# A selective-scan stack: the norm's factor spread by two transfers and multiplied in by GpSimd, the ffn's inner values in their own buffer, z projected a piece ahead

## The chip, the cores and the metric

The kernel runs on one core of a Trainium2 chip. A core has a matrix engine (TensorE, PE in the profile; its weight loads are PEld), a vector engine (VectorE, DVE), an engine for activation functions (ScalarE, ACT), a general one (GpSimd, POOL), and a fifth that only issues transfers (SyncE, SP). Each has its own queue of instructions and works through it in order; semaphores hold an instruction until what it needs is there. Sixteen DMA engines move data between HBM (DRAM) and the core's memory (SBUF); PE writes its results into PSUM. The metric is device time in microseconds (us).

## The reference, cut to what matters

The input is x of shape (2, 128, 64, 64). Four stages follow one another: the layers (this document's subject), two attentions over the picture, and a fusion of four scales. The layers, cut:

```python
t = (embed_w @ x + embed_b)                   # per image: 4096 tokens of 128 channels
for i in range(2):                            # two layers
    r = t
    t2 = layernorm(t) * ln_g[i] + ln_b[i]
    u, z = split(t2 @ in_w[i].T)              # 256 channels each
    u = silu(causal_conv4(u))
    dt, B, C = split(u @ xproj_w[i].T)        # 8, 16, 16 values
    dt = softplus(dt @ dt_w[i].T + dt_b[i])
    h[t] = exp(dt * A) * h[t - 1] + dt * u * B    # 256 x 16 states, along the tokens
    y = (h * C).sum(states) + u * ssm_D
    t = (y * silu(z)) @ mout_w[i].T + r
    r = t
    t2 = layernorm(t) * ln_g[i] + ln_b[i]
    t = gelu(t2 @ ffn_w1[i].T + ffn_b1) @ ffn_w2[i].T + ffn_b2 + r
x = x + (outc_w @ t + outc_b)
```

The norm is over the 128 channels: (x - mean) / sqrt(var + eps).

## The kernel before

**Tiling.** Channels lie on the 128 partitions and tokens along the free dimension, in pieces of 512. An item is one piece of one layer of one image: 2 images x 2 layers x 8 pieces = 32 items. The 256 x 16 states of an item are handled as 8 groups (NST) of four scans each, 128 partitions x 512 tokens per scan, so an item has 32 slots (NSL), one scan each. All data are fp32, and each matrix product appears in the trace as two matmul records.

**Order.** The order of all instructions is written out by hand. `slot` (L565) issues, for slot t: at the first slot of a group the transfers `dtb` that spread dt (L401) for three groups later, the product `pdu` (L406) for the next group, and in every second group the sums `py` (L445) of an earlier pair of groups; then the scan on DVE (L430); then on ACT the decay `da` for the scan four slots later (L419; four PSUM buffers); at the last slot of a group, after the scan, POOL copies the carry (L432) and multiplies h by C (L433, "the h product"), and DVE makes the next group's h out of B and pdu (`times_b`, L412). After that come the slot's entries of a list that `background` (L512) fills by hand with `at(slot, function, ...)`. pdu has one PSUM buffer (pool `l0bc`), so the product for the next group waits for times_b to have read the last. Since every engine keeps this order, an entry that waits holds up all that its engine has behind it.

**The list.** While step i scans item i, the list does for item n = i + 1 the input product with the convolution folded in (`pu`, slots 0 to 5), silu (11), `xproj` (13), the transfers `dr`, `bb`, `cb` that spread B and C over the partitions (14 and 22), `dtproj`, softplus (17) and dtu on POOL (18); for item i the product `pz` (slots 1 and 5, copied by ACT in 3 and 6); for item p = i - 1 the output `y_out`, gate and mix (7 to 11); for item q = i - 2 gelu (3), the ffn's second product (6, 7) and its sum. The products of the list share two PSUM buffers (tag `mm`).

**The norm.** Two norms go together in each step: the second norm of item p (result x2, for the ffn) and the first of item r = i + 2 (result xn). PE centres (12, 14), ACT squares (13, 15), PE makes the variances of both in a 2-row product (17), ACT adds eps (18, `ln_eps`), takes ln, exp and a square (19, `ln_rs`); one Newton step follows, with POOL and ACT in turn (20, 21). Then PE spreads each factor over the 128 partitions (`ln_spread`, L306, slot 27), DVE multiplies it in together with ln_g (`ln_scale`, L310, slot 28), and ACT adds ln_b (`ln_shift`, L323, slot 29). The ffn's first product `ph` (L478) and its copies into hid by ACT (L479) are in slots 30 and 31.

**Buffers.** h has a ring of five buffers (tag "h"), and hid, the ffn's inner values, takes one of the same ring in each step; for the last item it takes one of the attention's (tag "sc"). `xr`, the input for the last sum, has its own buffer.

Of the kernel before, what the change touches and what calls it, by code (L numbers as in the profile page):

```python
# [6 lines left out]
F32 = mybir.dt.float32  # L7
AF = mybir.ActivationFunctionType
ALU = mybir.AluOpType
# [6 lines left out]
P = 128  # L16
CH = 512
# [50 lines left out]
def tile_conv_seq(ctx: ExitStack, tc, x, consts, vecs, wemb, wlay, wconv, wdt, wqkv, wsmall, wms, out):  # L68
    nc = tc.nc
# [13 lines left out]
    def rows(ap):  # L83
        return ap.rearrange("p (h w) -> p h w", w=W)
# [19 lines left out]
    def v1(name, i=0):  # L104
        return vec[:, VEC[name] + i : VEC[name] + i + 1]

    def pick(row, k, m=P):

        return ident[:k, row : row + 1].to_broadcast([k, m])
# [6 lines left out]
    with tc.manual_schedule(), ExitStack() as s:  # L116
        wp = layers.enter_context(tc.tile_pool(name="l0w", bufs=1))
        spl = layers.enter_context(tc.tile_pool(name="l0t", bufs=1))
        mm = layers.enter_context(tc.tile_pool(name="l0mm", bufs=2, space=PSUM))
        yp = layers.enter_context(tc.tile_pool(name="l0y", bufs=1, space=PSUM))  # L120
        sp = scans.enter_context(tc.tile_pool(name="l0s", bufs=1, side="right"))
        bc = scans.enter_context(tc.tile_pool(name="l0bc", bufs=1, space=PSUM, side="right"))
        dap = scans.enter_context(tc.tile_pool(name="l0da", bufs=4, space=PSUM, side="right"))
        dp = s.enter_context(tc.tile_pool(name="l0d", bufs=2, space=bass.MemoryType.DRAM))
# [111 lines left out]
        NI, NST, NSL = len(items), 8, 32  # L236
        st = [{} for _ in items]
# [3 lines left out]
        def has(i):  # L241
            return 0 <= i < NI

        def vl(name, i, k=0):
            return v1(f"{name}{items[i][1]}", k)

        def tv(i):
            b, _, c = items[i]
            return xv(b, c)

        def mmt(name, p=P):
            return mm.tile([p, CH], F32, name=name, tag="mm")
# [27 lines left out]
                at = K_VS + 8 - k  # L280
                nc.tensor.matmul(var[:n], lhsT=kc[:, at : at + n], rhs=w["sq"][:, k, :], start=(k == 0), stop=(k == n - 1))

        def ln_eps(w, n):
            w["ve"] = spl.tile([2, CH], F32, name="ve", tag="ve")
            nc.scalar.activation(w["ve"][:n], w.pop("var")[:n], AF.Identity, bias=eps[:n])

        def ln_rs(w, n):
            w["rs"] = spl.tile([2, CH], F32, name="rs", tag="rs")
            nc.scalar.activation(w["rs"][:n], w["ve"][:n], AF.Ln)
            nc.scalar.activation(w["rs"][:n], w["rs"][:n], AF.Exp, scale=-0.5)  # L290
            w["nt"] = spl.tile([2, CH], F32, name="nt", tag="nt")
            nc.scalar.activation(w["nt"][:n], w["rs"][:n], AF.Square)

        def ln_newton(w, n):

            nt = w["nt"][:n]
            nc.gpsimd.tensor_tensor(nt, nt, w["ve"][:n], ALU.mult)
            nc.scalar.activation(nt, nt, AF.Identity, bias=c15[:n], scale=-0.5)

        def ln_step(w, n):  # L300
            rs = w["rs"][:n]
            nc.gpsimd.tensor_tensor(rs, rs, w["nt"][:n], ALU.mult)

        def ln_spread(w, k, n):
            w["pr", k] = mmt("pr")
            nc.tensor.matmul(w["pr", k], lhsT=pick(k, n), rhs=w["rs"][:n], start=True, stop=True)  # L306

        def ln_scale(w, k, i):
            cen = w["cen"][:, k, :]
            nc.vector.scalar_tensor_tensor(cen, cen, vl("ln_g", i), w.pop(("pr", k)), ALU.mult, ALU.mult)  # L310

        def ln_shift(w, k, i, second):
            if second:
                dst = st[i]["x2"] = spl.tile([P, CH], F32, name="x2", tag="x2")
            else:
                xn = st[i]["xn"] = sp.tile([P, KC - 1 + CH], F32, name="xn", tag="xn", bufs=2)
                if items[i][2] == 0:
                    nc.gpsimd.memset(xn[:, : KC - 1], 0.0)
                else:
                    nc.gpsimd.tensor_copy(xn[:, : KC - 1], prev_xn[0][:, CH : CH + KC - 1])  # L320
                prev_xn[0] = xn
                dst = xn[:, KC - 1 :]
            nc.scalar.activation(dst, w["cen"][:, k, :], AF.Identity, bias=vl("ln_b", i))  # L323


        def pu_taps(i, j, ks):
# [142 lines left out]
        def ffn_up(i, f):  # L469
            w = st[i]  # L470
            if f == 0:
                if i == NI - 1:
                    w["hid"] = spa.tile([P, 4, CH], F32, name="hid", tag="sc", bufs=3)
                else:
                    w["hid"] = sp.tile([P, 4, CH], F32, name="hid", tag="h", bufs=5)
            ph = mmt("ph")
            at = WL_W1 + f * P
            nc.tensor.matmul(ph, lhsT=wl[items[i][1]][:, at : at + P], rhs=w["x2"], start=True, stop=True)  # L478
            nc.scalar.activation(w["hid"][:, f, :], ph, AF.Identity, bias=vl("ffn_b1", i, f))  # L479
# [14 lines left out]
        def ffn_add(i):  # L494
            b, l, c = items[i]
            if l == NL - 1:
                xr = st[i]["xr"] = spl.tile([P, CH], F32, name="xr", tag="xr")
                nc.sync.dma_start(xr, x[b, :, c * RPC : (c + 1) * RPC, :].rearrange("c h w -> c (h w)"))
            nc.scalar.activation(tv(i), rows(st[i].pop("pf")), AF.Identity, bias=vl("ffn_b2", i))

# [11 lines left out]
        def background(i):  # L512

            todo = [[] for _ in range(NSL)]

            def at(t, f, *a):
                todo[t].append((f, a))

            n, p, q, r = i + 1, i - 1, i - 2, i + 2
            if has(q):  # L520
                at(3, gelu, q)
                at(6, ffn_down, q, (0, 1)), at(7, ffn_down, q, (2, 3)), at(9, ffn_add, q)
                at(11, out_mm, q), at(12, out_add, q)
            if has(p):
                at(7, y_out, p, 1), at(7, gate, p)
                at(9, mix_out, p), at(11, mix_add, p)
            if has(n):
                at(0, pu_taps, n, 0, (0, 1)), at(1, pu_taps, n, 0, (2, 3)), at(2, pu_out, n, 0)
                at(3, pu_taps, n, 1, (0, 1)), at(4, pu_taps, n, 1, (2, 3)), at(5, pu_out, n, 1)
                at(13, xproj, n), at(14, xproj_out, n), at(14, spread_bc, n, 0), at(22, spread_bc, n, 1)  # L530
                at(15, dtproj, n, 0), at(16, dtproj, n, 1), at(17, soft_plus, n), at(18, dt_end, n)
            if has(i):
                at(1, pz_mm, i, 0), at(3, pz_out, i, 0)
                at(5, pz_mm, i, 1), at(6, pz_out, i, 1)
            if has(i) or has(n):
                at(11, silu, i, n)
            if i == -1:
                at(1, load_rest), at(7, prepare, 1), at(9, through_out)
                for k in range(3):
                    at(8 + k, fold, k), at(23, fold_out, k)  # L540
                at(19, spread_dtu, 0), at(26, times_b, 0)
            pair = [(k, second) for k, second in ((p, True), (r, False)) if has(k)]
            if has(r):
                at(10, embed, r), at(11, embed_out, r)
            w, m = {}, len(pair)
            for k, (it, second) in enumerate(pair):
                at(12 + 2 * k, ln_centre, w, k, it)
                at(13 + 2 * k, ln_square, w, k, it)
                at(27, ln_spread, w, k, m), at(28, ln_scale, w, k, it)
                at(29, ln_shift, w, k, it, second)  # L550
            if pair:
                at(17, ln_var, w, m), at(18, ln_eps, w, m), at(19, ln_rs, w, m), at(20, ln_newton, w, m), at(21, ln_step, w, m)
            if has(p):
                for f in range(4):
                    at(30 + f // 2, ffn_up, p, f)
            if has(i):
                at(24, y_out, i, 0)
            return todo

        eps = wp.tile([P, 1], F32, name="eps")  # L560
# [21 lines left out]
        for i in range(-2, NI):  # L582
            todo = background(i)
            for t_ in range(NSL):
                slot(i, todo, t_)
        todo = background(NI)
        for t_ in range(8):
            slot(NI, todo, t_)
# [15 lines left out]
        spa = s.enter_context(tc.tile_pool(name="ata", bufs=1, reuse_waits="tile", side="right"))  # L604
# [297 lines left out]
        for k in range(8, 2 * NSL):  # L902
            if k == NSL:
                todo = background(NI + 1)
            for _ in range(int(beside[k - 8]) if k - 8 < len(beside) else 0):
                next(steps, None)
            slot(NI + k // NSL, todo, k % NSL)
# [4 lines left out]
        sp = s.enter_context(tc.tile_pool(name="ats", bufs=1, reuse_waits="tile"))  # L912
        psa = s.enter_context(tc.tile_pool(name="atpa", bufs=2, reuse_waits="tile", space=PSUM))
        psm = s.enter_context(tc.tile_pool(name="atpm", bufs=1, reuse_waits="tile", space=PSUM))
        for now in range(NALL + LAG + 8):
            r, u = divmod(now, NU)
            w = now % 8
# [64 lines left out]
    with ExitStack() as s, tc.manual_schedule():  # L982
        sp = s.enter_context(tc.tile_pool(name="mss", bufs=1, reuse_waits="tile"))
# [11 lines left out]
        for ti in range(NS):  # L995
            src = spr[:, ti, :].unsqueeze(2).to_broadcast([P, NH, HD])
# [27 lines left out]
        eps = sp.tile([P, 1], F32, name="eps")  # L1024
# [9 lines left out]
        for si in (2, 3):  # L1034
            wgt[si] = sp.tile([P, SCALES[si]], F32, name=f"wgt{si}")
            for k in range(SCALES[si]):
                w = (k + 0.5) / SCALES[si] - 0.5
# [5 lines left out]
        NI = len(items)  # L1043
        st = [{} for _ in items]
# [433 lines left out]
```

## Time and profile before

| what | us |
|---|---|
| median of 3 runs | 4975.6 (4974.84 to 4981.31) |
| the profiled execution's own time | 4975.69 |
| its span, first to last instruction | 4973.9 |
| layers, first scan to last scan (66.7 to 2094) | 2027 |
| PE busy in it | 1818 |
| DVE busy in it | 1883 |
| ACT busy in it | 1467 |
| POOL busy in it | 1428 |
| mean granted TensorE clock | 0.949 |

The profile is one execution, told by several views. A line of the timeline has start, length, engine, source line, operation, output and inputs with their shapes and the count; in brackets is the idle time of the engine before it, and what ended it. The chain of waits is followed back from the last instruction, at each step to what released it. "issue" is time in which nothing was waited for that the profile shows. A window has, after its length, the busy times of PE, PEld, DVE, ACT and POOL, with counts, then the granted clock of PE as a share of full speed, the share of the DMA engines in use, and GB/s. Line numbers are those of the kernel before.

### The profile page before, as it was taken

The numbers are of one execution on the slowest core, as the hardware profiler recorded it, in microseconds if no ns is written. First come the engines' busy times: TensorE is split into PE (matmuls) and PEld (weight loads), VectorE is DVE, ScalarE is ACT, GpSimd is POOL, SyncE is SP. The second block draws the span as 40 slices with busy tenths as digits, with TensorE's granted clock in tenths as the row PEclk, the third lists the DMA queues.
The fourth block names the chain that finished last, engine by engine and source line by source line (L and its number), as shares of the span: only waits on it lengthen the run. The fifth ranks groups of instructions, "written<-read, shape, count | busy, mean of one in ns | idle before, by whom it ended". The sixth has DMA issues, their size and how long they took to land.

```text
span 4973.9 us, 48435 instructions
## 1 busy us (share of the span) xinstructions
PE 4643.1 (93%) x14634; PEld 2218.0 (45%) x14634; DVE 3975.5 (80%) x4155; ACT 2361.8 (47%) x3225; POOL 2331.1 (47%) x1974
## 2 busy tenths in 40 slices
PE   6899999999988899899999999999999999999997
PEld 2222222222222222266667766666666666333332
DVE  6999999999999999878886677767766775667775
ACT  4677777777777777632222232233333332323332
POOL 3777776676777777613332233333333332334231
PEclk8888898988999989899999999999999999999998
DMA  6333332223333333214444444444444443000000
GB/s 163 68 67 68 69 69 67 67 67 71 69 69 69 71 73 71 69 36 126 113 111 123 113 109 115 122 99 111 114 101 98 114 112 83 3 7 7 7 5 9
DMA packets 242485, 386.28 MB, mean 78 GB/s; under 512 B 88608, under 2 KB 89136, under 8 KB 233776
## 3 DMA queue, kind: packets, MB, share of 16 engines
q1 hardware_dynamic: 193072, 316.01, 26.1%
q10 hardware_dynamic: 49152, 67.17, 5.4%
q8 instruction: 117, 1.92, 0.2%
q14 instruction: 144, 1.18, 0.1%
HBM read 101.09 MB, written 13.37 MB: 23 GB/s over the span
## 4 chain that ended last, share of the span: by engine, by line
PE 46%; POOL 25%; issue 12%; DVE 8%; DMA 4%; SPq 3%; ACT 3%; ACTq 0%; POOLq 0%; DVEq 0%
POOL h L433 19%; PE pq L780 13%; PE po L830 13%; DVE tr L810 3%; SPq L821 3%; DMA pt<-tr 3%; PE pa L677 2%; PE pf L1135 2%; PE pqkv L1162 2%; PE pw L1221 1%; POOL dtu L393 1%; POOL z L456 1%; PE pb L677 1%; PE pfus L1286 1%; PE psc L1186 1%
## 5 line engine op out<-in xcount | busy, mean ns | idle before, releaser
L817 POOL COPY pt<-tr 32x512 f32<-32x512 f32 x1024 | 644.7, 630 | 1410.8 <-DVE tr L810 700.7
L430 DVE TENSOR_TENSOR_SCAN h<-da,carry,h 128x512 f32<-128x512 f32 x1024 | 1241.6, 1265 | 65.1 <-ACT da L419 36.2
L433 POOL TENSOR_TENSOR h<-h,cb 128x2048 f32<-128x2048 f32 x256 | 1160.9, 4535 | 20.8
L780 PE MATMUL pq<-k,q 128*128 128x512 f32 x2048 | 963.4, 593 | 12.5 <-DVE sc L785 12.5
L830 PE MATMUL po<-pt,vt 128*128 128x256 f32 x4096 | 965.6, 379 | 3.5 <-POOL pt L817 3.5
L795 ACT ACTIVATE sc<-sc,nm 128x2048 f32<-128x2048 f32 x256 | 510.5, 1995 | 886.8 <-DVE nm L791 656.4
L830 PEld LDWEIGHTS po<-pt,vt 128*128 128x128 f32 x4096 | 777.9, 190 | 309.5 <-issue 227.5
L785 DVE TENSOR_SCALAR_CACHE_REDUCE sc<-pq 128x1024 f32<-128x1024 f32 x512 | 624.8, 1222 | 333.8 <-PE pq L780 311.7
L419 ACT ACTIVATE da<-dtb,am 128x512 f32<-128x512 f32 x1024 | 681.4, 684 | 221.3 <-DVE h L430 205.6
L412 DVE TENSOR_TENSOR h<-bb,pdu 128x2048 f32<-128x2048 f32 x256 | 581.4, 2271 | 85.4 <-PE py L445 28.3
L810 DVE STREAM_TRANSPOSE tr<-sc 128x2048 f32<-128x2048 f32 x256 | 591.6, 2311 | 65.7 <-DMA pt<-tr 59.3
L445 PE MATMUL py<-h,sel 128*32 128x512 f32 x2048 | 513.6, 645 | 1.8 <-POOL h L433 1.8
L780 PEld LDWEIGHTS pq<-k,q 128*128 128x128 f32 x2048 | 382.2, 190 | 291.5 <-issue 247.4
L406 PE MATMUL pdu<-dtu,fsel 128*128 128x512 f32 x512 | 327.8, 727 | 99.5 <-DVE h L412 97.5
L445 PEld LDWEIGHTS py<-h,sel 128*32 128x32 f32 x2048 | 115.6, 118 | 418.7 <-issue 413.1
L333 PE MATMUL pu<-xn,wu 128*128 128x512 f32 x512 | 245.9, 614 | 10.0 <-ACT u L339 8.3
L406 PEld LDWEIGHTS pdu<-dtu,fsel 128*128 128x128 f32 x512 | 96.6, 215 | 307.4 <-DVE h L412 180.5
L432 POOL COPY carry<-h 128x4 f32<-128x4 f32 x256 | 47.8, 187 | 390.3 <-DVE h L430 386.2
L1228 DVE TENSOR_TENSOR ov<-v,pw 128x2048 f32<-128x2048 f32 x64 | 146.2, 2284 | 65.1 <-PE pw L1221 65.1
L1162 PE MATMUL pqkv<-f,ws 128*128 128x512 f32 x384 | 188.8, 617 | 3.0 <-DVE prod L1179 2.3
L1232 POOL TENSOR_TENSOR ov<-ov 128x2048 f32<-128x2048 f32 x16 | 72.6, 4536 | 237.0 <-DVE ov L1228 237.0
L393 POOL TENSOR_TENSOR dtu<-dt,u 128x1024 f32<-128x1024 f32 x32 | 75.1, 2348 | 199.1 <-ACT dt L387 199.1
(265 smaller groups left out, 5152.4 us busy)
## 6 DMA issues: line engine op xcount, KB each, us to landing
pt<-tr SPq DMA_DIRECT2D x2048, 64.0 KB, 2.0
dtb<-dt SPq DMA_DIRECT2D x1024, 64.0 KB, 2.0
pt<-tr ACTq DMA_DIRECT2D x1024, 64.0 KB, 2.1
bb<-dr SPq DMA_DIRECT2D x128, 256.0 KB, 4.5
cb<-dr SPq DMA_DIRECT2D x128, 256.0 KB, 4.6
uw<-ufold SPq DMA_DIRECT2D x12, 576.0 KB, 4.4
uw<-dkept SPq DMA_DIRECT2D x20, 288.0 KB, 3.1
xt<-in_x SPq DMA_DIRECT2D x16, 256.0 KB, 4.8
```

The costliest lines, as they stand in the source:

```text
L406: nc.tensor.matmul(pdu, lhsT=four(s_ % 4), rhs=st[i]["dtu"][:, s_ // 4, :], start=True, stop=True)
L412: nc.vector.tensor_tensor(h, st[i]["bc", 0], pdu.unsqueeze(1).to_broadcast([P, 4, CH]), ALU.mult)
L419: nc.scalar.activation(da, st[i]["dtb", s_], AF.Exp, scale=am[items[i][1]][:, j, gg, m : m + 1])
L430: nc.vector.tensor_tensor_scan(h[:, m, :], da, h[:, m, :], carries[b, l][:, j, gg, m : m + 1], ALU.mult, ALU.add)
L433: nc.gpsimd.tensor_tensor(h, h, st[i]["bc", 1], ALU.mult)
L445: nc.tensor.matmul(py[r : r + 32, :], lhsT=sel, rhs=st[i]["h", s_ + k][:, m, :], start=(m == 0), stop=(m == 3), tile_position=(0, r),)
L780: nc.tensor.matmul(pq[:, i, :], lhsT=sta["q", r, grp][:, it * P : (it + 1) * P], rhs=sta["k"][:, at : at + CH], start=True, stop=True)
L785: nc.vector.tensor_scalar(dst, pq, 1.0, None, ALU.mult, ALU.max, accum_out=sta["mx"][:, c2 : c2 + 1])
L795: nc.scalar.activation(sc, sc, AF.Exp, bias=nm, scale=scale, accum_out=sm[:, hh : hh + 1])
L810: nc.vector.transpose(tr, sta.pop(("sc", r, blk, hh)).rearrange("p (t r f) -> p r t f", r=NB, f=32))
L817: nc.gpsimd.tensor_copy(dst, src)
L830: nc.tensor.matmul(sta["po", r, grp], lhsT=sta["vt"][:, jt, :], rhs=rhs, start=(jt == 0), stop=(jt == N // P - 1))
```

## The change

- `ln_eps` goes into `ln_rs`: ACT's four operations are issued together in slot 18. ve and nt lie in sq, which is free by then. The whole Newton step is in slot 19.
- `ln_spread` on PE goes. `ln_out` (slot 21) writes the factors (2 x 512) to DRAM; `ln_in` (slot 23) reads them back, each repeated for 128 partitions, into sq. Both are issued by SP.
- `ln_scale` is a product on POOL, without ln_g, in slots 25 and 27. ln_g is applied by ACT as the scale of `ln_shift`, for both norms in slot 28.
- hid has a buffer of its own in the pool of the layers. xr shares the buffer of x2.
- pz is made one item ahead: for n = i + 1, in slots 24 and 26, with its copies in 25 and 27.

```diff
-        def ln_eps(w, n):
-            w["ve"] = spl.tile([2, CH], F32, name="ve", tag="ve")
-            nc.scalar.activation(w["ve"][:n], w.pop("var")[:n], AF.Identity, bias=eps[:n])
-
         def ln_rs(w, n):
-            w["rs"] = spl.tile([2, CH], F32, name="rs", tag="rs")
-            nc.scalar.activation(w["rs"][:n], w["ve"][:n], AF.Ln)
-            nc.scalar.activation(w["rs"][:n], w["rs"][:n], AF.Exp, scale=-0.5)
-            w["nt"] = spl.tile([2, CH], F32, name="nt", tag="nt")
-            nc.scalar.activation(w["nt"][:n], w["rs"][:n], AF.Square)
+            ve, nt = w["sq"][:n, 0, :], w["sq"][:n, 1, :]
+            rs = w["rs"] = spl.tile([2, CH], F32, name="rs", tag="rs")
+            nc.scalar.activation(ve, w.pop("var")[:n], AF.Identity, bias=eps[:n])
+            nc.scalar.activation(rs[:n], ve, AF.Ln)
+            nc.scalar.activation(rs[:n], rs[:n], AF.Exp, scale=-0.5)
+            nc.scalar.activation(nt, rs[:n], AF.Square)
 
         def ln_newton(w, n):
-            nt = w["nt"][:n]
-            nc.gpsimd.tensor_tensor(nt, nt, w["ve"][:n], ALU.mult)
+            ve, nt, rs = w["sq"][:n, 0, :], w["sq"][:n, 1, :], w["rs"][:n]
+            nc.gpsimd.tensor_tensor(nt, nt, ve, ALU.mult)
             nc.scalar.activation(nt, nt, AF.Identity, bias=c15[:n], scale=-0.5)
-
-        def ln_step(w, n):
-            rs = w["rs"][:n]
-            nc.gpsimd.tensor_tensor(rs, rs, w["nt"][:n], ALU.mult)
-
-        def ln_spread(w, k, n):
-            w["pr", k] = mmt("pr")
-            nc.tensor.matmul(w["pr", k], lhsT=pick(k, n), rhs=w["rs"][:n], start=True, stop=True)
-
-        def ln_scale(w, k, i):
+            nc.gpsimd.tensor_tensor(rs, rs, nt, ALU.mult)
+
+        def ln_out(w, n):
+            w["rd"] = dp.tile([2, CH], F32, name="rd", tag="rd")
+            nc.sync.dma_start(w["rd"][:n], w["rs"][:n])
+
+        def ln_in(w, n):
+            src = w["rd"][:n].rearrange("(o k) f -> o (k f)", o=1)
+            nc.sync.dma_start(w["sq"][:, :n, :].rearrange("p k f -> p (k f)"), src.to_broadcast([P, n * CH]))
+
+        def ln_scale(w, k):
             cen = w["cen"][:, k, :]
-            nc.vector.scalar_tensor_tensor(cen, cen, vl("ln_g", i), w.pop(("pr", k)), ALU.mult, ALU.mult)
+            nc.gpsimd.tensor_tensor(cen, cen, w["sq"][:, k, :], ALU.mult)
...
-            nc.scalar.activation(dst, w["cen"][:, k, :], AF.Identity, bias=vl("ln_b", i))
+            nc.scalar.activation(dst, w["cen"][:, k, :], AF.Identity, bias=vl("ln_b", i), scale=vl("ln_g", i))
...
-                if i == NI - 1:
-                    w["hid"] = spa.tile([P, 4, CH], F32, name="hid", tag="sc", bufs=3)
-                else:
-                    w["hid"] = sp.tile([P, 4, CH], F32, name="hid", tag="h", bufs=5)
+                w["hid"] = spl.tile([P, 4, CH], F32, name="hid", tag="hid")
...
-                xr = st[i]["xr"] = spl.tile([P, CH], F32, name="xr", tag="xr")
+                xr = st[i]["xr"] = spl.tile([P, CH], F32, name="xr", tag="x2")
...
-            if has(i):
-                at(1, pz_mm, i, 0), at(3, pz_out, i, 0)
-                at(5, pz_mm, i, 1), at(6, pz_out, i, 1)
+                at(24, pz_mm, n, 0), at(25, pz_out, n, 0)
+                at(26, pz_mm, n, 1), at(27, pz_out, n, 1)
...
-                at(27, ln_spread, w, k, m), at(28, ln_scale, w, k, it)
-                at(29, ln_shift, w, k, it, second)
+                at(25 + 2 * k, ln_scale, w, k)
+                at(28, ln_shift, w, k, it, second)
             if pair:
-                at(17, ln_var, w, m), at(18, ln_eps, w, m), at(19, ln_rs, w, m), at(20, ln_newton, w, m), at(21, ln_step, w, m)
+                at(17, ln_var, w, m), at(18, ln_rs, w, m), at(19, ln_newton, w, m)
+                at(21, ln_out, w, m), at(23, ln_in, w, m)
```

## The prediction

> **What bounds the kernel now.** I read the page first, for the shares, then the chain of waits, then one round of the layers in the timeline, then the clock in windows, then the DMA issues. I look at the layers alone (up to about 2094 us of the span); the change touches nothing after them. From the page, the engines and the chain:
>
> ```profile
> PE 4643.1 (93%) x14634; PEld 2218.0 (45%) x14634; DVE 3975.5 (80%) x4155; ACT 2361.8 (47%) x3225; POOL 2331.1 (47%) x1974
> ...
> PE 46%; POOL 25%; issue 12%; DVE 8%; DMA 4%; SPq 3%; ACT 3%; ACTq 0%; POOLq 0%; DVEq 0%
> ```
>
> POOL is idle half of the time and yet holds a quarter of the chain: a loop passes through it. The chain in order of time (start, length, what), in the round of item 15:
>
> ```profile
> 1059.28 2.35 POOL dtu L393
> ...
> 1061.84 4.55 POOL h L433
> 1066.39 1.24 POOL nt L297
> ...
> 1068.28 0.68 ACT da L419
> ...
> 1068.98 1.26 DVE h L430
> ...
> 1072.61 2.19 DVE h L412
> 1074.80 0.04 issue
> 1074.85 2.08 PE pdu L406 x2
> 1076.92 5.21 PE py L445 x16
> 1082.13 3.82 PE ph L478 x8
> 1085.95 0.86 PE pdu L406 x2
> 1086.81 3.43 PE pu L333 x8
> 1090.24 0.87 PE pz L346 x2
> ```
>
> This is one round of a loop. Call D the start of dtu. POOL does dtu, the h product and nt; ACT's nt lets the next decay go; three scans and times_b follow on DVE; and only then may PE start pdu, because pdu has one PSUM buffer. From there PE works without a gap through py, ph, pu, pz, ffn, mix, centre and xproj; in the timeline softplus then ends 6.0 to 6.6 us after xproj, and the next dtu starts. The dtu starts are 172.67 and 2009.27 us for items 1 and 30: 29 rounds of 63.3 us, 61.7 to 65.1 each. In every round times_b of group 7 ends 15.5 us after D (call that point B) and pdu starts 0.05 us after it; what varies is PE after B. DVE is busy some 60 us of a round; its stalls (about 4.5 us) follow the loop rather than make it.
>
> ACT in the same round, from its timeline:
>
> ```profile
> 1067.65 0.72 ACT L298 ACTIVATE nt<-nt,c 2x512 f32<-2x512 f32 x1 [2.68 <-POOL nt L297]
> 1079.94 0.71 ACT L323 ACTIVATE xn<-cen,vec 128x512 f32<-128x512 f32 x1
> 1083.23 0.69 ACT L479 ACTIVATE hid<-ph,vec 128x512 f32<-128x512 f32 x1 [2.00 <-PE ph L478]
> ```
>
> xn is ready 5.8 us after B, and hid waits for PE: the norm has about 2 us to spare. The windows show the clock (the column after POOL) and the DMA share after it:
>
> ```profile
> 1056.30:1059.80 3.50, 2.27 (x6) 0.55 (x6) 3.19 (x2) 3.45 (x5) 0.52 (x1) 0.99 1.01 227
> 1059.80:1063.20 3.40, 3.40 (x6) 0.54 (x6) 3.38 (x4) 3.30 (x6) 3.32 (x3) 0.51 0.99 209
> 1070.00:1080.20 10.20, 8.70 (x14) 1.98 (x15) 10.10 (x10) 4.97 (x9) 9.22 (x4) 0.50 0.23 53
> 1080.20:1124.60 44.40, 43.16 (x116) 14.39 (x113) 39.61 (x29) 34.83 (x49) 26.21 (x13) 1.00 0.17 42
> ```
>
> A window with 1.23 us of idle PE is followed by one at half clock, and full clock returns only after a stretch of unbroken work. The second thing to see: while bb, cb and dtb land, all DMA engines are taken (0.99), at 209 GB/s. The issues, with the median time to landing:
>
> ```profile
> bb<-dr SPq DMA_DIRECT2D x128, 256.0 KB, 4.5
> cb<-dr SPq DMA_DIRECT2D x128, 256.0 KB, 4.6
> uw<-ufold SPq DMA_DIRECT2D x12, 576.0 KB, 4.4
> ```
>
> **The change, part by part**, for one round.
>
> *Removed from DVE and PE.* Two scale instructions on DVE (0.73 each) and two spreading products on PE (3.59 us cold, at 1069.76, between the loop's own pieces). Both lie off the loop, or before B where PE waits anyway: 0.
>
> *hid in its own buffer, ve and nt in sq, xr in x2's buffer.* The h ring keeps five buffers. DVE's waits at slots 31 and 7 (1.21 and 1.01 us for py, at 1082.23 and its like at 1032.67) go. They are shadows of PE's chain: y_out behind them waits for the same py. 0 on the loop. xr's load now waits for x2's last reader, a third of a round earlier: 0.
>
> *z a piece ahead.* The two pz in the PE stretch cost 0.94 each there (1090.08 to the next product at 1091.02); they move to slots 24 and 26, where PE idles before B: -1.9. Their copies on ACT go to slots 25 and 27, where ACT waits 2.9 and 1.8 us for scans: 0.
>
> *ve, ln, exp, square together; the Newton step a slot earlier.* The decay for scan 23 now stands behind ln, exp and square: 1.9 us later. More weighs that ACT's nt, which waits for POOL until 1067.65, now stands before the decay of scan 24 and not of scan 25. POOL's dtu, h and nt are the same, so scan 24 starts where scan 25 did, D + 9.7. From there: scan and y_out 1.9, three scans 3.55, times_b 2.26, so B is at D + 17.4 instead of D + 15.5: +1.9. The late scan 23 is covered (its times_b ends at D + 9 to 10).
>
> *Two transfers.* rs is ready at D + 10.4 (POOL 1069.71). ln_out is queued on SP ahead of cb, so cb, which went out at D + 3.8, now waits for rs too. It is needed only by the next item's first h product: 0. ln_out's 4 KB is taken at the 1.6 us of dr<-dbl (64 KB), landing at D + 12.1; cb's four issues take 1.9, so ln_in goes out at D + 12.75. It writes 512 KB. Alone it takes the 4.4 of uw<-ufold (576 KB): D + 17.15. Behind cb's 1 MB on full DMA engines, 1.5 MB at 209 GB/s take 7.5 us from D + 11.8: D + 19.4. The latter is nearer, since cb goes out just before it on the same queue. Call the landing B + 2.0; ends B - 0.25 and B + 2.6. The next dtb sit behind it on SP, needed 8 us later than they land: 0.
>
> *POOL's scale.* POOL's 2x512 product takes 1.26, and 128x1024 and 128x2048 (2.35, 4.54) lie on a line that gives 1.26 for 128x512. POOL would be free at B - 2.2; it waits, then scale 1.26, carry and h product 4.81, scale 1.26: B + 9.3. ACT's slot 28 holds both shifts, and in order behind them stand two decays and the first hid: 0.7 + 1.3 + 0.7, so hid ends at B + 12.05. PE has done py at B + 7.0 (rounds: 6.1 to 7.8) and two ph at B + 8.9; the third needs the buffer that hid empties (two PSUM buffers): PE waits 3.2 us, at the low end of ln_in 0.9, at the high end 3.8. pu needs xn (B + 10) anyway.
>
> *Clock.* By the row of 1056.30, a wait of this kind drops PE to half clock. The next two windows of 3.4 us hold the rest of the wait and some 4 to 5 us of work that then run at half: +1.9, between 0 and 3.4.
>
> Sum for a round: -1.9 + 1.9 + 3.2 + 1.9 = +5.1; 30 rounds: +153. At the head, item 0's norm sits on the path (rs 21.29, pu 25.10): out 1.6, in 4.4 and POOL 1.26 beside 3.0 for product and scale, and loads before them on SP: +7 (between 4 and 15). Tail: the last pr (2131.91) waits 6 us behind other products, which covers the transfers. The profiled execution took 4975.69 us, 1.8 around its 4973.9 span; the median is 4975.6, so no correction. 4975.7 + 160 = 5136.
>
> **Two rules beside the rows.** The Trainium skill, "DMA: Bandwidth & Descriptors", section "Anatomy of one DMA", gives 2.0 us plus bytes over 436 GB/s for a transfer (fitted on the GpSimd path). As an estimate ln_in would take 3.2 us, land at B - 1.45, and PE would wait nothing: 4983 by this sum. The rows show 209 GB/s with the engines full, so I keep the rows. The skill's "TensorE: Matmul & The Clock Gate", "Why this matters for your kernels", asks for no idle gap over about 3 us. By it most waits of 3.2 us or less would leave the clock alone: 5136 - 57 = 5079. The row with 1.23 us idle and 0.51 after it speaks against that.
>
> **Rivals.** (1) Faster: DVE is the true bound. Then 1.4 of scales and the waits of 1.2 and 1.0 come off each round: -3.6 x 30 = -108, 4868. For it: DVE is busy 93% of the layers. Against it: pdu follows times_b by 0.05 us in every round while DVE waits for py and pdu. It decides if PE's gaps between pdu and xproj turn out to be cover. A smaller form, PE kept at full clock by pz, would give up to -2.4 a round (py at B + 4.6), 4904; PE is idle over 5 us before B, against it. (2) The transfer is hidden: ln_in lands by B - 1.2, so that hid ends by B + 8.9, with the second ph. The round is then -1.9 + 1.9 = 0, with the head 4983. Against it: cb on the same queue. (3) ln_in is not queued behind cb and the clock holds: +0.9 a round, 5003 to 5010; this is the low end of my forecast.
>
> **How the numbers follow.** Within 0.2% (10 us) this kernel can't be told from no change. Chances: forecast with its low end (rival 3 included) 0.80; rival 2 0.09; rival 1 with its smaller form 0.11. Rival 2 ends on both sides of +0.2%, mostly within. So faster 0.12, same 0.07, slower 0.81. Upper end: 3.8 + 3.4 = 7.2 a round and 13 at the head, 5205. Lower end: rival 3 and part of rival 2, 4990. Outside lie rival 1 and what is over 7.2 a round, together under 0.2.
>
> **What would show it.** POOL's scale waits about 4 us for the DMA sq<-rd in each round; ACT's xn ends 9 to 10 us after B; PE's ph has an idle time of about 3 us before the third product, put down to ACT hid or xn; B lies 17.4 after D; rounds of 68 us; half clock in more windows after B. The prediction is wrong if sq<-rd lands before POOL's h product of group 5 ends, or if rounds fall to 60 us with DVE without gaps.

## The result, and the profile after

The changed kernel takes 5106.4 us (median of 4 runs, 5100.46 to 5109.29), the kernel before 4977.3 beside it (4974.84 to 4981.31): a ratio of 1.0257, with a 95% interval of 1.0239 to 1.0275. That is 129 us slower, where 160 were forecast. The profiled execution has a span of 5098.6 us, 124.7 more than before. From its page, the engines and the chain's shares:

```profile
PE 4605.2 (90%) x14506; PEld 2223.2 (44%) x14506; DVE 3939.6 (77%) x4091; ACT 2368.8 (46%) x3225; POOL 2405.5 (47%) x2038
...
PE 46%; POOL 19%; issue 12%; DVE 8%; DMA 6%; ACT 4%; SPq 3%; ACTq 0%; DVEq 0%; POOLq 0%
POOL h L431 13%; PE pq L775 13%; PE po L825 13%; DMA sq<-rd 3%; DVE tr L805 3%; SPq L816 3%; DMA pt<-tr 2%; PE pa L672 2%; PE pf L1130 2%; PE pqkv L1157 2%; POOL cen L308 1%; PE pw L1216 1%; PE pb L672 1%; POOL dtu L391 1%; PE pfus L1281 1%
```

PE and DVE have less to do than before and the program is longer, so both wait more. A line that before didn't have stands in the chain, DMA sq<-rd: ln_in, the transfer that spreads the norm's factor. One round of it, from the chain in order of time (start, length, what); D is at 984.73:

```profile
984.73 2.34 POOL dtu L391
...
991.78 1.27 POOL sq L294
...
993.08 0.73 ACT sq L295
...
993.87 1.26 POOL rs L296
...
995.27 0.12 SPq L300
...
997.30 6.30 DMA sq<-rd
...
1003.67 1.26 POOL cen L308
...
1005.15 1.88 POOL h L431
...
1009.62 1.29 POOL cen L308
```

The Newton step ends at D + 10.4, as forecast. Then SP issues ln_out, the four parts of cb and ln_in; ln_in goes out at D + 12.6 and lands 6.3 us later, at D + 18.9. This B is at 1002.05 (the pdu below starts 0.14 after it), so the landing is B + 1.55 (B + 1.5 in the mean of the 29 rounds below). POOL can scale x2's centred values only now, and xn's only after the next h product. The same round on PE and on ACT, from their timelines (in brackets the idle time before, and what ended it):

```profile
1002.19 2.05 PE L404 MATMUL pdu<-dtu,fsel 128*128 128x512 f32 x2 [5.17 <-DVE h L410]
1004.17 5.13 PE L443 MATMUL py<-h,sel 128*32 128x512 f32 x16
1009.23 1.98 PE L473 MATMUL ph<-x,wl 128*128 128x512 f32 x4
1013.61 3.36 PE L473 MATMUL ph<-x,wl 128*128 128x512 f32 x4 [2.39 <-ACT hid L474]
```

```profile
1004.97 0.81 ACT L321 ACTIVATE x<-cen,vec 128x512 f32<-128x512 f32 x1 [0.81 <-POOL cen L308]
1010.94 0.81 ACT L321 ACTIVATE xn<-cen,vec 128x512 f32<-128x512 f32 x1 [5.16 <-POOL cen L308]
1011.66 1.28 ACT L417 ACTIVATE da<-dtb,am 128x512 f32<-128x512 f32 x2
1012.89 1.24 ACT L474 ACTIVATE hid<-ph,vec 128x512 f32<-128x512 f32 x2
```

PE needs x2, which is there at 1005.8. It has made the first two ph by 1011.2, and waits 2.39 us for a PSUM buffer. ACT could empty it at once, but in its queue the shift of xn stands first, and that one waits 5.16 us for POOL. So PE waits for a value that it doesn't use for the ph. Over the layers, from the table of waits (total, times, longest):

```profile
ACT xn L321 <- POOL cen L308: 134.4, 27, 5.2
POOL cen L308 <- DMA sq<-rd: 118.2, 31, 4.7
...
PE ph L473 <- ACT hid L474: 72.3, 29, 3.4
...
DVE h L428 <- POOL carry L426: 19.7, 3, 6.6
```

Before, POOL and ACT had neither of the first two waits, and PE's third was not among the long ones. The windows of the round (length, busy PE, PEld, DVE, ACT, POOL, granted clock, DMA share, GB/s):

```profile
998.00:1004.70 6.70, 2.51 (x4) 0.69 (x6) 6.60 (x6) 3.32 (x6) 2.89 (x2) 0.68 0.94 234
```

```profile
1007.20:1014.10 6.90, 4.51 (x15) 1.32 (x12) 4.95 (x4) 3.16 (x6) 6.82 (x5) 0.99 0.05 11
1014.10:1017.50 3.40, 3.40 (x5) 1.35 (x4) 1.92 (x2) 1.79 (x4) 2.99 (x3) 0.50 0.25 57
1017.50:1020.90 3.40, 3.40 (x9) 1.52 (x8) 2.54 (x2) 1.99 (x4) 3.40 (x1) 1.00 0.09 20
```

In the first the DMA engines are full (0.94): cb's 1 MB and ln_in's 512 KB. The second holds the wait of 2.39 us at full clock; the third has PE busy throughout and half the clock.

Taken over the 29 rounds from item 1 to item 30 (means, us; the parts are cut at the events that the prediction named, and add up to the round):

| | before | after | difference |
|---|---|---|---|
| D to B | 15.50 | 17.40 | +1.90 |
| PE idle from B to the end of xproj | 0.09 | 2.70 | +2.61 |
| PE busy from B to the end of xproj | 41.45 | 40.66 | -0.79 |
| end of xproj to the next D | 6.29 | 6.29 | 0 |
| round | 63.33 | 67.05 | +3.72 |

From B to the end of xproj the clock is at half for 7.48 us instead of 4.80; over whole rounds it is 13.97 instead of 12.60, since it is 1.3 us less in the rest of the round. The 29 rounds make 107.9 of the 124.7 us; the first of these D is 13.5 later (186.2 for 172.7), and what follows the last D is 3.3 longer.

### The profile page after: what moved, and what is told of

The parts are those of the page before. It is cut to its first block, busy times and chain, and to the rows that moved or that the text cites. A ratio compares the mean times of both kernels' runs of the same rounds, so it can differ in the third digit from the quotient of the medians.

```text
span 5098.6 us, 48298 instructions
## 1 busy us (share of the span) xinstructions
PE 4605.2 (90%) x14506; PEld 2223.2 (44%) x14506; DVE 3939.6 (77%) x4091; ACT 2368.8 (46%) x3225; POOL 2405.5 (47%) x2038
## 4 chain that ended last, share of the span: by engine, by line
PE 46%; POOL 19%; issue 12%; DVE 8%; DMA 6%; ACT 4%; SPq 3%; ACTq 0%; DVEq 0%; POOLq 0%
POOL h L431 13%; PE pq L775 13%; PE po L825 13%; DMA sq<-rd 3%; DVE tr L805 3%; SPq L816 3%; DMA pt<-tr 2%; PE pa L672 2%; PE pf L1130 2%; PE pqkv L1157 2%; POOL cen L308 1%; PE pw L1216 1%; PE pb L672 1%; POOL dtu L391 1%; PE pfus L1281 1%
## 5 line engine op out<-in xcount | busy, mean ns | idle before, releaser
L404 PE MATMUL pdu<-dtu,fsel 128*128 128x512 f32 x512 | 339.4, 750 | 223.3 <-DVE h L410 221.3
L473 PE MATMUL ph<-x,wl 128*128 128x512 f32 x256 | 149.6, 714 | 72.3 <-ACT hid L474 72.3
```

The lines of the kernel that those rows point to most:

```text
L404: nc.tensor.matmul(pdu, lhsT=four(s_ % 4), rhs=st[i]["dtu"][:, s_ // 4, :], start=True, stop=True)
```

## The experiments

My theory after the result: two queues make the cost. ln_in stands behind cb on the DMA queue and so lands late; the shift of xn stands ahead of hid's copies on ACT and hands the delay to PE, which then loses clock as well. The rivals were that POOL's product or the transfer is dear by itself, wherever it stands; that the late B costs what the table gives it; and that DVE is the true bound. All kernels below compute the whole of the reference. In the column of rounds, before has 63.33 and after 67.05. PE idle, PE busy and half clock are taken from B to the end of xproj, as above, and so wherever they are named below.

| kernel | median, us | ratio to before (95%) | round | D to B | PE idle | PE busy | half clock |
|---|---|---|---|---|---|---|---|
| after, xn's shift behind hid | 5007.7 | 1.0057 (1.0041 to 1.0074) | 63.95 | 17.42 | 0.61 | 39.64 | 5.00 |
| after, cb behind ln_in | 4986.9 | 1.0019 (1.0010 to 1.0028) | 63.23 | 17.34 | 0.42 | 39.16 | 4.37 |
| after, Newton's slots as before | 5131.6 | 1.0308 (1.0293 to 1.0324) | 68.11 | 15.51 | 4.86 | 41.44 | 10.98 |
| after, z as before | 5174.1 | 1.0393 (1.0377 to 1.0408) | 69.59 | 17.41 | 2.95 | 42.94 | 8.09 |
| after, both as before | 5184.0 | 1.0415 (1.0397 to 1.0432) | 70.14 | 15.52 | 4.40 | 43.94 | 10.96 |
| before, with z ahead | 4949.6 | 0.9944 (0.9929 to 0.9959) | 62.48 | 15.50 | 0.45 | 40.21 | 5.06 |
| before, with the Newton order | 5033.3 | 1.0109 (1.0094 to 1.0124) | 65.09 | 17.42 | 0.08 | 41.29 | 4.45 |
| before, with hid's own buffer | 4977.0 | 0.9999 (0.9989 to 1.0008) | 63.40 | 15.52 | 0.12 | 41.47 | 4.81 |
| before, z ahead and Newton later | 5003.4 | 1.0049 (1.0034 to 1.0064) | 64.32 | 15.12 | 0.31 | 42.57 | 7.91 |
| after, three moves | 4932.3 | 0.9910 (0.9895 to 0.9925) | 61.64 | 15.51 | 0.37 | 39.46 | 4.57 |
| before, z ahead and sooner | 4929.5 | 0.9904 (0.9889 to 0.9919) | 61.76 | 15.50 | 0.51 | 39.43 | 4.41 |
| before, z sooner, hid's own buffer | 4920.2 | 0.9886 (0.9870 to 0.9903) | 61.61 | 15.51 | 0.21 | 39.59 | 5.18 |

### The queue on ACT: xn's shift behind hid's copies

```diff
-                at(28, ln_shift, w, k, it, second)
+                if second:
+                    at(28, ln_shift, w, k, it, second)
...
                 for f in range(4):
                     at(30 + f // 2, ffn_up, p, f)
+                    if f == 1 and has(r):
+                        at(30, ln_shift, w, len(pair) - 1, r, False)
...
```

> The changed kernel with one thing moved: ACT's shift that makes xn is issued after the first two copies into hid (slot 30) and no longer ahead of them (slot 28). Theory (ACT, held in order by the late xn, empties the product's buffer too late, and PE waits): hid then waits only for PE, xn is there about 10.3 us after B and pu asks for it at about 11.8; the wait of PE (2.6 a round) and the half clock it brings (about 1.1) go, -3.7 x 29 rounds: about 5000 us, rounds of 63.3. Rival (POOL's two added products and the added 512 KB slow the round by themselves): the wait moves elsewhere, 5090 to 5110.

5007.7 us. The transfer is as late as ever, and costs nearly nothing in the rounds. From the waits of this kernel:

```profile
POOL cen L308 <- DMA sq<-rd: 127.5, 32, 5.0
...
ACT xn L321 <- POOL cen L308: 1.0, 2, 0.7
...
DVE h L428 <- POOL carry L426: 20.2, 3, 6.8
```

POOL waits even more than in after (127.5 for 118.2 us), and xn comes 10.39 us after B instead of 9.66; yet PE's idle time falls from 2.70 to 0.61 and the round by 3.10. So what PE waited for was the place in ACT's queue. What is left in the rounds sits in three of the 29, in which a new layer or image begins: they take 69.1 us in mean (63.9 before), the other 26 take 63.36 (63.27 before). In those three the first scan waits for the carry's memset, which stands behind POOL's scales and h products. In all other rounds nothing in the transfer or in POOL's product has to be on PE's path. The rest of the 30 us over before is the head (first D at 186.8).

### The DMA queue: cb behind ln_in

```diff
-                at(13, xproj, n), at(14, xproj_out, n), at(14, spread_bc, n, 0), at(22, spread_bc, n, 1)
+                at(13, xproj, n), at(14, xproj_out, n), at(14, spread_bc, n, 0), at(24, spread_bc, n, 1)
```

> The changed kernel with cb's four transfers issued after ln_in (slot 24) and no longer ahead of it (slot 22). Theory (ln_in takes 6.3 us because 1 MB of cb lies ahead of it on full DMA engines): it lands in 4.4 to 5, about 0.7 us before B and not 1.5 after; hid is 2.2 earlier, PE's wait falls from 2.6 to about 0.5, -2.2 to -3.2 a round with the clock: 5015 to 5045 us. Rival (a transfer to 128 partitions has its time by itself): landing still about 6 us after the issue, at most -0.5 a round, 5090 to 5106.

4986.9 us, a larger gain than expected. The chain and the waits of this kernel:

```profile
951.30 3.86 DMA sq<-rd
```

```profile
POOL cen L308 <- DMA sq<-rd: 28.6, 31, 4.5
...
PE ph L473 <- ACT hid L474: 3.3, 8, 0.6
```

The same 512 KB land in 3.86 us in the round shown instead of 6.30; in the mean of the 29 rounds it is 4.1 (3.6 to 4.5) instead of 6.3. They also go out 0.8 us sooner, at D + 11.8, since SP issues cb's four parts after them and not before. Together that moves the landing from B + 1.5 to B - 1.5. ACT's order need not be touched: the ph wait 3.3 us in all, not 72.3, and half clock falls to 4.37 us a round. Each of the two queues alone decides over nearly all of the cost in the rounds: moving one takes 3.1 of the 3.72 us off, moving the other 3.8. That also shows that cb had the time to stand behind. What is left over before is the head (first D at 183.5) and, with 4.9 us, the stretch after the last D.

### Each of the two other moves undone

Newton's slots as before (the four functions split again, the buffers of the change kept):

```diff
...
-                at(17, ln_var, w, m), at(18, ln_rs, w, m), at(19, ln_newton, w, m)
+                at(17, ln_var, w, m), at(18, ln_eps, w, m), at(19, ln_rs, w, m), at(20, ln_newton, w, m), at(21, ln_step, w, m)
```

> The changed kernel with the order of the Newton step as before (eps 18, ln, exp and square 19, then 20 and 21). B comes back to D + 15.5. Theory (the late hid is fixed to the factor rs, which POOL gives at the same time in both orders): PE starts 1.9 us sooner and then waits 1.9 us longer in ph, no gain: 5095 to 5110 us. Rival (the terms add up, as the prediction's sum has them): -1.9 x 29 = -55, about 5050 us.

5131.6 us, 25 slower than after, and neither number. B is back at D + 15.51, 1.9 sooner, and PE reaches the ph sooner, only to wait longer. From PE's timeline:

```profile
1030.62 3.78 PE L478 MATMUL ph<-x,wl 128*128 128x512 f32 x4 [4.95 <-ACT hid L479]
```

xn comes at about the same time in both kernels, D + 27.2 here (15.51 + 11.73) and D + 27.1 in after (17.40 + 9.66), since POOL and the queue set it, not B. The wait grows by 2.16, which is more than the 1.9 given, and half clock by 3.5 us, beside which PE is busy 0.78 longer with the same work. A masked delay is what the theory said; that undoing it costs, through the clock, it didn't.

z as before:

```diff
-                at(24, pz_mm, n, 0), at(25, pz_out, n, 0)
-                at(26, pz_mm, n, 1), at(27, pz_out, n, 1)
+            if has(i):
+                at(1, pz_mm, i, 0), at(3, pz_out, i, 0)
+                at(5, pz_mm, i, 1), at(6, pz_out, i, 1)
```

> The changed kernel with z's products back in slots 1 and 5 of the item's own step. Theory (they lie behind PE's wait, in its gapless stretch, 0.94 us each): +1.9 x 29 = +55, about 5160 us, rounds of 68.9. Rival (the moved products gained nothing since the loop is set elsewhere): 5100 to 5110 us.

5174.1 us, 68 slower than after, the theory's direction and 14 us over its number: 2.54 a round, 2.28 of it busy PE, of which the two pz are 1.88. Both undone, which leaves the transfers, POOL's product and the buffers:

> The changed kernel with both z and the Newton step as before: of what moves the time, the transfers and POOL's product are left alone. Theory (hid's time is fixed to rs, and what the two other parts do adds to it as in their single runs): 5106 + 25 + 68, 5190 to 5210 us, that is, the transfers cost more alone than the whole change, and z gives a third of it back. Rival (the parts hide one another): 5130 to 5175 us.

5184.0 us, 6 under the theory's range. The transfers with their scale and the buffers alone cost 208 us, more than the whole change.

### Each of the other parts alone, in the kernel before

z ahead, in the slots of the change:

```diff
-            if has(i):
-                at(1, pz_mm, i, 0), at(3, pz_out, i, 0)
-                at(5, pz_mm, i, 1), at(6, pz_out, i, 1)
+                at(24, pz_mm, n, 0), at(25, pz_out, n, 0)
+                at(26, pz_mm, n, 1), at(27, pz_out, n, 1)
```

> The kernel before with z's products alone moved one item ahead (slots 24 and 26). Theory (PE's gapless stretch from B to xproj is on the loop): -0.94 x 2 x 29 = -55, about 4922 us, rounds of 61.4. Rival (DVE or POOL is the bound): 4965 to 4980 us.

4949.6 us, half of the gain expected. PE's timeline of this kernel shows the rest:

```profile
988.35 1.88 PE L346 MATMUL pz<-xn,wl 128*128 128x512 f32 x4
993.49 1.09 PE L306 MATMUL pr<-rs,kc 2*128 2x512 f32 x2 [3.25 <-ACT z L349]
995.33 1.86 PE L306 MATMUL pr<-rs,kc 2*128 2x512 f32 x2 [0.76 <-ACT z L349]
997.13 2.08 PE L406 MATMUL pdu<-dtu,fsel 128*128 128x512 f32 x2
```

Both pz take the two `mm` buffers, and ACT copies them out only in slots 25 and 27. The spreading products pr, which this kernel still has, wait for them and hold pdu to 997.13, 0.9 after B (996.22). So the removal of pr, which the prediction put at 0, is part of what lets z gain in the change.

The Newton order, with `ln_eps` and `ln_rs` in slot 18, `ln_newton` and `ln_step` in 19:

```diff
-                at(17, ln_var, w, m), at(18, ln_eps, w, m), at(19, ln_rs, w, m), at(20, ln_newton, w, m), at(21, ln_step, w, m)
+                at(17, ln_var, w, m), at(18, ln_eps, w, m), at(18, ln_rs, w, m), at(19, ln_newton, w, m), at(19, ln_step, w, m)
```

> The kernel before with the Newton step's order of the changed kernel alone (eps, ln, exp and square in 18, the rest in 19). Theory (scan 24 and no longer scan 25 waits for ACT's nt): B at D + 17.4, +1.9 x 29 = +55, about 5032 us, rounds of 65.2. Rival (the delay is covered by DVE's other waits): 4970 to 4985 us.

5033.3 us, as expected. B goes from D + 15.50 to D + 17.42, and nothing masks it here.

hid in a buffer of its own, ve and nt in sq, xr in x2's buffer (the lines for ve and nt are left out here):

```diff
...
-                if i == NI - 1:
-                    w["hid"] = spa.tile([P, 4, CH], F32, name="hid", tag="sc", bufs=3)
-                else:
-                    w["hid"] = sp.tile([P, 4, CH], F32, name="hid", tag="h", bufs=5)
+                w["hid"] = spl.tile([P, 4, CH], F32, name="hid", tag="hid")
...
-                xr = st[i]["xr"] = spl.tile([P, CH], F32, name="xr", tag="xr")
+                xr = st[i]["xr"] = spl.tile([P, CH], F32, name="xr", tag="x2")
```

> The kernel before with the buffers of the changed kernel alone: hid in its own, ve and nt in sq, xr in x2's. Theory (DVE's waits for an h buffer are shadows of PE's chain): the waits at slots 31 and 7 go and come back at y_out and pdu, 4970 to 4985 us. Rival (DVE is the bound): up to -2.2 a round, about 4913 us.

4977.0 us beside 4977.3: no difference. From the waits of the kernel before, and of this one:

```profile
DVE h L412 <- PE py L445: 28.3, 27, 2.4
DVE h L412 <- PE pdu L406: 21.0, 44, 0.8
```

```profile
DVE h L410 <- PE pdu L404: 70.0, 44, 2.5
```

The waits of DVE that this edit was forecast to remove went, and as long a wait for pdu came in their place: in the 29 rounds DVE is idle 4.3 us a round before and 4.5 here. They weren't on the loop.

The other direction for Newton, together with z ahead: `ln_newton` in slot 22 and `ln_step` in 23, so that ACT's nt would not stand before a decay that B needs.

```diff
-                at(17, ln_var, w, m), at(18, ln_eps, w, m), at(19, ln_rs, w, m), at(20, ln_newton, w, m), at(21, ln_step, w, m)
+                at(17, ln_var, w, m), at(18, ln_eps, w, m), at(19, ln_rs, w, m), at(22, ln_newton, w, m), at(23, ln_step, w, m)
```

> The kernel before with z's products one item ahead and the Newton step two slots later (22 and 23 in place of 20 and 21). Theory: ACT's nt then stands behind the decays of scans 25 and 26, so that POOL's products are off the loop and B is set by the decay of scan 23: D + 14.3 to 15.4 in place of 15.5, 0.1 to 1.2 a round beside the 1.9 of z: 4890 to 4920 us, if the factor still reaches PE in time. Rival (the later factor delays xn and with it ph): about 4925 us or over.

5003.4 us: the rival. B does come sooner (15.12), but pr now waits for the late factor, from 951.34 + 1.88 of pz to 956.93, and pdu stands behind it until 960.64. Half clock goes to 7.91 us a round.

### What follows for the kernel

Three moves that the runs point to, all in the changed kernel: cb behind ln_in, xn's shift behind hid's first copies, Newton's slots as before. With them `fold_out`, the stores of ufold, goes behind ln_in in the head. The diff leaves out the lines that make xn's shift anew, as above, and those that split the four functions.

```diff
...
-                at(13, xproj, n), at(14, xproj_out, n), at(14, spread_bc, n, 0), at(22, spread_bc, n, 1)
+                at(13, xproj, n), at(14, xproj_out, n), at(14, spread_bc, n, 0), at(24, spread_bc, n, 1)
...
-                    at(8 + k, fold, k), at(23, fold_out, k)
+                    at(8 + k, fold, k), at(27, fold_out, k)
...
-                at(28, ln_shift, w, k, it, second)
+                if second:
+                    at(28, ln_shift, w, k, it, second)
...
-                at(17, ln_var, w, m), at(18, ln_rs, w, m), at(19, ln_newton, w, m)
+                at(17, ln_var, w, m), at(18, ln_eps, w, m), at(19, ln_rs, w, m), at(20, ln_newton, w, m), at(21, ln_step, w, m)
```

> The changed kernel with the three orders moved together: cb behind ln_in, the shift of xn behind the first two copies into hid, the Newton step in its old slots; and, for the head alone, the stores of the folded weights behind ln_in (slot 27 in place of 23). Theory: with no wait of PE left to hide it, the earlier B now counts: PE starts 15.5 us after D, waits for nothing, and z's 1.9 stay saved: rounds of 61.4 to 62, the head 5 to 10 us shorter than in the changed kernel: 4925 to 4950 us. Rival (the three moves overlap, or the transfer still decides): 4985 us, as with cb's move alone.

4932.3 us, 0.9% under the kernel before: against cb's move alone, D to B is 1.83 shorter and PE's idle time no longer (0.37 for 0.42), and the round loses 1.59. The same Newton slots cost 25 us in after; here the table suggests that they gain, since no wait later in the round grows by what B is sooner. But no run has cb and xn moved with the change's Newton slots, so the shares of the moves aren't measured one by one. The first scan starts at 74.9 us instead of after's 87.3.

And the kernel before with z ahead, but the pz early enough that ACT has emptied the buffers when pr comes:

```diff
-            if has(i):
-                at(1, pz_mm, i, 0), at(3, pz_out, i, 0)
-                at(5, pz_mm, i, 1), at(6, pz_out, i, 1)
+                at(21, pz_mm, n, 0), at(22, pz_out, n, 0)
+                at(22, pz_mm, n, 1), at(23, pz_out, n, 1)
```

> The kernel before with z's products one item ahead in slots 21 and 22 and their copies in 22 and 23, so that they lie ahead of pr and not between pdu and pr. Theory (with z in 24 to 27, pr waited for ACT's copies of z and ended 0.9 us after B): pr ends before B again, and all of the 1.9 is gained: rounds of 61.4, 4918 to 4930 us. Rival (z earlier delays pdu or the decays): 4945 us or over.

4929.5 us: the round loses 1.57, against 0.85 with the slots of the change. With hid's own buffer added to it:

> The same, and the buffers of the changed kernel (hid in its own, ve and nt in sq, xr in x2's). Theory: as long as PE's stretch decides, the buffers bring nothing: within 5 us of the run without them, 4918 to 4930 us. Rival (with PE's stretch shorter, DVE's waits for h begin to count): 5 to 30 us faster than without.

4920.2 us, 1.1% under before and the best of all. From its page:

```profile
PE 4619.9 (94%) x14634; PEld 2218.8 (45%) x14634; DVE 3968.4 (81%) x4155; ACT 2351.4 (48%) x3225; POOL 2328.8 (47%) x1974
...
PE 50%; POOL 17%; DVE 12%; issue 8%; DMA 6%; SPq 4%; ACT 3%; DVEq 0%; ACTq 0%; POOLq 0%
```

Against before, the chain has moved from POOL to PE and DVE. Both kernels keep the norm on PE and DVE, so what gains here is z's place and not the transfers. hid's buffer, which alone brought nothing, takes 9.3 us off the median here: more than the theory's 5, and within the rival's 5 to 30. The rounds hold 4.4 of it (0.15 x 29), and the stretch from the last D to the last scan is 4.0 shorter (79.6 us for 83.6). Whether that is DVE's waits for h, as the rival has it, isn't shown.

## Why the prediction was right

The direction and the mechanism were right, and the time was inside the range; the forecast was 30 us too high. By its own steps:

- *B from D + 15.5 to D + 17.4, +1.9.* Measured 15.50 to 17.40, and alone, in the kernel before, 15.50 to 17.42, which there costs 56 us. The argument by ACT's order (nt before the decay of scan 24) gave it to 0.02 us. But as a term of a sum it failed: in after it hides behind the wait for xn, and undoing it makes the kernel 25 us slower. The later B is, the shorter is the wait behind it, because the wait ends at a time that is fixed from D. The forecast added the two as if they were independent, which came out right only because the wait was reckoned from the late B.
- *PE's wait in the ph, +3.2.* Its place, its releaser and the chain behind it (ln_in behind cb, POOL's scale, ACT's slot 28) were as said, and the two runs that undo one queue each show them as the cause. Its size was 2.6. The transfer was put at B + 2.0, from 1.5 MB at 209 GB/s; it landed at B + 1.5 in mean (1.1 to 2.3), and the window of the round shown has 234 GB/s.
- *The clock, +1.9.* Right in kind, too large: 2.68 us more of half clock from B to the end of xproj, which cost 1.1 of busy PE (the difference of -0.79 less the -1.88 of z).
- *z, -1.9.* In the kernel before, the two pz take 1.88 of the PE time from B to the end of xproj. But what the move is worth depends on what stands beside it: 0.85 alone, 1.57 alone and sooner, 2.54 within the change.
- *hid's buffer, scales, pr: 0.* The buffer alone is 0. The wait at 1082.23, which the prediction reads as one for py, the trace puts down to POOL's carry. No run takes out pr or the scales by itself; but with pr kept, z in the slots of the change is worth 0.85, so pr isn't nothing once z stands in those slots.
- *Head, +7; tail, 0.* Measured 13.5 and 3.3. The head is the term that was most off. Item 0's norm, the one that the prediction counted, makes the first dtu 5.3 later (61.77 for 56.47). The rest comes from the norm of item 1 in step -1, where SP has six stores of ufold to issue ahead of ln_in. The stores, then the two transfers in the chain, POOL and DVE:

```profile
72.72 1.22 SPq L229 DMA_DIRECT2D ufold<-uhi  x1
...
75.39 0.32 SPq L304 DMA_DIRECT2D sq<-rd  x1
```

```profile
22.75 4.08 DMA sq<-rd
...
75.39 10.39 DMA sq<-rd
```

```profile
85.85 1.26 POOL L308 TENSOR_TENSOR cen<-cen,sq 128x512 f32<-128x512 f32 x1 [16.70 <-DMA sq<-rd]
```

```profile
87.34 4.87 DVE L428 TENSOR_TENSOR_SCAN h<-da,carry,h 128x512 f32<-128x512 f32 x4 [17.56 <-POOL carry L426]
```

  Each brings the factor of one norm, 256 KB. The second takes 10.4 us, POOL waits 16.7, and the first scan starts 20.6 us late (87.3 for 66.7), because the carry's memset stands behind POOL's scale. The prediction named "loads before them on SP" without working them out, and it did not ask what POOL had queued behind its scale. With cb alone behind ln_in the head's loss is 10.8 (first D at 183.5); in the kernel with three moves, where the stores stand behind too, it is 2.0 (174.7). Of the tail's 3.3 none lies in the layers: from the last D to the attention's first product pq it is 184.6 us, before 185.6. From there to the end, where the change has no part, the fourteen profiled executions take 2777 to 2787 us; what makes them differ isn't settled here.

The sum for a round was 5.1 and came to 3.72: 0.6 of the difference from the wait and 0.8 from the clock. The forecast also took 30 rounds of it, where 29 lie between the first D and the last.

The rivals: that DVE is the bound fell with hid's buffer alone (0 for waits taken from DVE). That the transfer is hidden had the right price, but its condition, a landing by B - 1.2, isn't met in the changed kernel: it was put at 4983, and with cb out of its way, where the landing is at B - 1.5, the kernel takes 4986.9. That the transfer isn't queued and the clock holds was put at 5003 to 5010, with a landing at B - 0.25; cb behind it came out lower, since ln_in then goes out at D + 11.8 and not at D + 12.75, and takes 4.1 us and not the 4.4 taken from uw.

The two rules. The Trainium skill, "DMA: Bandwidth & Descriptors", section "Anatomy of one DMA", would give, as an estimate, 3.2 us for these 512 KB; measured 4.1 in mean with cb behind it, and 6.3 with cb's 1 MB ahead. So the estimate is 0.9 short without cb and 3.1 short with it: the formula has no term for a queue, and here the queue decided. "TensorE: Matmul & The Clock Gate", section "Why this matters for your kernels", asks only for no gap over about 3 us. The windows above disagree: a wait of 2.39 us was followed by 3.4 us at a clock of 0.50.

The parts don't add. Starting from before, the transfers cost 6.81 a round, z on top of them gives back 2.03, and the Newton order a further 1.06 (rounds of 70.14, 68.11, 67.05). Alone in before, that Newton order costs 1.76 and z saves 0.85.

## What to carry to other kernels

When a value moves from an engine to a transfer, follow what each in-order queue has behind the one that waits for it: here neither the transfer nor the product on POOL was dear, but two places in two queues (512 KB behind 1 MB that nobody needed yet, and a shift for later ahead of a copy that PE needed now) cost 2.6 us of waiting a round, and clock beside it. Price the parts of a change together, as the loop that they share: a delay that costs 56 us alone saved 25 us where another wait came after it. And price the head by itself, since its queues hold other work than those of a steady round.

## What the runs showed of the hardware that was not expected

- A wait costs more than its length, by the clock that follows it. With Newton's slots as before, PE's idle time from B to the end of xproj was 2.16 longer than in after, its time at half clock 3.5 longer, and PE was busy 0.78 longer with the same work.
- Queueing on the DMA engines is worth 2.2 us for 512 KB: 4.1 us in mean clear of cb, 6.3 behind it. In the head 256 KB took 4.08 us the first time, and 10.39 behind cb and the stores of ufold.
- At the three changes of layer or image the first scan waits for the carry's memset on POOL, up to 6.6 us (the last line of after's waits), where before it waited 2.5 at most: POOL's wait for a transfer reaches DVE by way of an instruction of 0.12 us.
